# Layer 3 of a four-layer network: two outputs packed into one fp16 product of signs, another form of PReLU, and layer 2's norm folded into weights

## The chip, the cores and the metric

The kernel runs on one core of a Trainium2 chip. A core has five engines that run side by side and wait for one another through semaphores: TensorE (PE, matrix products into PSUM), VectorE (DVE), ScalarE (ACT), GpSimd (POOL) and SyncE (SP), which here issues nearly all the transfers. The metric is the device time of one execution in microseconds (us). Before the change it is 2025.56 us, the median of three runs from 2024.20 to 2026.01.

## What is computed

The input x has 8 images of 512 channels and 32 x 32 = 1024 pixels, in fp32. Four layers follow one another, each with a residual: an attention normed by the largest singular value (layer 0), a softmax attention over 512 channels (layer 1), one over 128 channels with a batch norm at its end (layer 2), and a binary convolution with PReLU (layer 3). The change touches the end of layer 2 and the whole of layer 3:

```python
# layer 2, its end: att is [n, 128, 1024]
z = einsum('oc,ncq->noq', Z_w, att)
inv = bn_gamma / sqrt(bn_var + 1e-5)
x = z * inv + (bn_beta - bn_mean * inv) + x

# layer 3; every vector has one value per channel
a = sign(x + rsign_bias)
scale = mean(abs(W), axis=1)
y = einsum('bchw,oc->bohw', a, sign(W) * scale)
bn = bn_gamma * (y - bn_mean) * rsqrt(bn_var + 1e-5) + bn_beta
t = bn + x - pr_shift
out = where(t > 0, t, pr_slope * t) + pr_bias
```

In layer 3 both operands of the product are signs, so that before scaling every output is a whole number between -512 and 512.

## The kernel before

Everything is laid out with channels on the 128 partitions: an image is four tiles of 128 channels (index cc or oc, 0 to 3) by 1024 pixels, and most work goes by halves of 512 pixels (index h). A product's output is a PSUM tile of 128 x 512, called `bank`; the main part has 8 of them.

A start of some 215 us loads the images, does layer 0's products (L1013), forms weights (`filler`, a list of small steps that is laid between the steps of the singular-value iteration, `chain`; in this part TensorE's order is written out by hand) and brings the first image into layer 1. Then `fast` is called for each of the 8 images in turn. For one image it does:

- `scores1`, `make_v`, `values1`: layer 1. The products follow the Strassen-Winograd scheme in `seven`, seven products in place of eight, so that each big product needs sums of quarters of its operands first. For the scores these sums are of u, made by `sums_of` on VectorE (L286 to L289, four additions of 128 x 1024).
- `project2`, `scores2` and the products with L799: layer 2's attention.
- `close2`: the product with Z (L632) into a bank, times the inverse of the softmax sums on VectorE (z, L637), the batch norm on ScalarE (L638, scale and bias per partition), the residual on GpSimd (L642).
- `leave`: layer 3. For each half, four Sign activations (L650) write the bf16 tile `sg`; for each of four output tiles four bf16 products (L660) fill one bank, and then come the scale and residual on VectorE (t, L670), Relu on ScalarE (up, L673), min(t + cb, 0) on VectorE (L674), slope times that plus up on VectorE (L675), the last bias on ScalarE (L678) and the store (L679).

The steps of `make_u` for the next image are handed out one by one between the steps of layers 2 and 3 (`fill`), so that TensorE has work while layer 2 and 3 wait for the other engines. After the last of them come the sums of u, and then the next image's `scores1`. The last image has no successor and so no such steps.

Outside the part with TensorE's order by hand, a planner lays out each engine's instructions: it takes them by their place in the program and by when, by its own costs, they could start. The program then holds one list for each engine, gone through in that order: in the trace, an instruction that waits holds up what is behind it.

Temporary tiles come from the pool `small`, three buffers for each tag: `half_a` holds t of layer 3 (and att, and the temporaries of `values1`), `half_b` holds z and `up`. A buffer is free again when its last reader is done; for a stored tile this is when the transfer has landed. In `leave` before the change the stored tile is `up`, in `half_b`.

Weights for layer 3 are made early: `sign_weights` writes the signs of W as bf16 (L958) and sums the absolute values, `scale_signs` makes the per-channel vectors sa3 (scale), cb3 (bias before PReLU), inv2 and bb2 (layer 2's norm). `biases` makes the biases of layer 1 by products with one column (L1089, L1104).

Of the kernel before, what the change touches and what calls it, by code (L numbers as in the profile page):

```python
# [8 lines left out]
F32 = mybir.dt.float32  # L9
BF16 = mybir.dt.bfloat16  # L10
I32 = mybir.dt.int32
# [60 lines left out]
GUARD = 1e20  # L72
RATIO = 8.0
EBUFS = 8


@with_exitstack
def kernel(
# [146 lines left out]
    gm = [keep.tile([P, 3, P], F32, tag=f"gm{j}", name=f"gm{j}") for j in range(NPAIR)]  # L225
    sw3 = wpool.tile([P, CC, C], BF16, tag="sw3", name="sw3")
    sa3 = const.tile([P, CC], F32, tag="sa3", name="sa3")
# [399 lines left out]

    def close2(env, xt, att, h, r=None):

        for oc in range(CC):  # L630
            ps = bank()
            mm(out=ps, lhsT=sbw["z"][:, bass.ts(oc, P)], rhs=att, start=True, stop=True)  # L632
            z = env["small"].tile([P, HF], F32, tag="half_b", name="z")
            if r is None:
                nc.scalar.copy(z, ps)
            else:
                nc.vector.tensor_tensor(z, ps, r, ALU.mult)  # L637
            nc.scalar.activation(  # L638
                z, z, AF.Identity, bias=bb2[:, oc : oc + 1], scale=inv2[:, oc : oc + 1]
            )  # L640
            xs = xt[:, oc, half(h)]
            nc.gpsimd.tensor_tensor(xs, xs, z, ALU.add)  # L642

    def leave(env, xt, dst, fill=lambda h: None):

        small = env["small"]
        for h in range(NH):
            sg = env["e"].tile([P, CC, HF], BF16, tag="e", name="sg")
            for cc in range(CC):
                nc.scalar.activation(  # L650
                    sg[:, cc, :],
                    xt[:, cc, half(h)],
                    AF.Sign,
                    bias=col("L3_conv_rsign_bias", cc),
                )
            for oc in range(CC):
                cb = cb3[:, oc : oc + 1]
                ps = bank()
                for cc in range(CC):
                    mm(  # L660
                        out=ps,
                        lhsT=sw3[:, cc, bass.ts(oc, P)],
                        rhs=sg[:, cc, :],
                        start=cc == 0,
                        stop=cc == CC - 1,
                    )

                t = small.tile([P, HF], F32, tag="half_a", name="t3")
                up = small.tile([P, HF], F32, tag="half_b", name="up3")
                nc.vector.scalar_tensor_tensor(  # L670
                    t, ps, sa3[:, oc : oc + 1], xt[:, oc, half(h)], ALU.mult, ALU.add
                )
                nc.scalar.activation(up, t, AF.Relu, bias=cb)  # L673
                nc.vector.tensor_scalar(t, t, cb, 0.0, ALU.add, ALU.min)  # L674
                nc.vector.scalar_tensor_tensor(  # L675
                    t, t, col("L3_conv_pr_slope", oc), up, ALU.mult, ALU.add
                )
                nc.scalar.activation(up, t, AF.Identity, bias=col("L3_conv_pr_bias", oc))  # L678
                nc.sync.dma_start(out=dst[:, oc, half(h)], in_=up)  # L679
                fill(h)  # L680

# [68 lines left out]
    def fast(env, n, hb, ua):  # L750
# [45 lines left out]
        for h in range(NH):  # L796
# [12 lines left out]
            if h == 0:  # L809
                r = inverse_sums(env, esum, B + n)  # L810
        close2(env, xt, atts[0], 0, r[:, 0, :])
        fill()
        close2(env, xt, atts[1], 1, r[:, 1, :])
        fill(2)
# [138 lines left out]
    def sign_weights():  # L953

        w3 = sbw["w3"]
        absw = a1.tile([P, 2, C], F32, tag="absw", name="absw")
        for cc in range(CC):
            nc.scalar.activation(sw3[:, cc, :], w3[:, cc, :], AF.Sign)  # L958
            nc.scalar.activation(absw[:, min(cc, 1), :], w3[:, cc, :], AF.Abs)
            if cc:  # L960
                nc.vector.tensor_tensor(absw[:, 0, :], absw[:, 0, :], absw[:, 1, :], ALU.add)
        return absw[:, 0, :]

    def scale_signs(total):
# [21 lines left out]
        nc.vector.tensor_tensor(bb2, inv2, vec("L2_conv_bn_mean"), ALU.mult)  # L986
        nc.vector.tensor_tensor(bb2, vec("L2_conv_bn_beta"), bb2, ALU.subtract)


# [201 lines left out]
    def filler():  # L1191

        yield from natural("v", "k")
        load_w("p", w_p, [P, CC, C], a1, tag="v")
        yield from gram(jl, 2, ht_pair[jl], gtl)
        yield from product(nat["q"], nat["k"], wu)
        cols2 = [slice(0, C // 2), slice(C // 2, C)]
        weights["u"] = sums_of(quarters_of(wu, chunks, cols2), [su[:, i] for i in range(3)])
        for j in rest:
            yield from grams(j)  # L1200
        yield from biases()
        yield from product(nat["v"], sbw["p"], wo)
        weights["o"] = sums_of(quarters_of(wo, chunks, cols2), [so[:, i] for i in range(3)])
# [176 lines left out]
    with tc.If(again > 0):  # L1380
        with (
            ExitStack() as stack,
            tc.tile_pool(name="gbig", bufs=1) as big,
            tc.tile_pool(name="gepool", bufs=2) as epool,
            tc.tile_pool(name="gsmall", bufs=1) as small,
        ):
# [50 lines left out]
```

## Time and profile before

| What | Value |
|---|---|
| time, median of 3 runs | 2025.56 us (2024.20 to 2026.01) |
| profiled execution, span | 2025.1 us, mean granted clock 0.988 |
| TensorE busy | 97% of the span |
| VectorE, ScalarE, GpSimd busy | 54%, 28%, 13% |
| transfers | 67.03 MB, 33 GB/s on average |
| one image, from the first layer-3 product to that of the next | about 219 us in the later images (1579.85 to 1798.51) |

The page of the profile has parts: the busy time of each engine; the span in 40 slices with the busy share in tenths and the clock granted to TensorE; the transfer queues; the chain of waits that ended last, with the share of each engine and line in it; and the groups of instructions, each with its line, engine, operation, output and inputs, count, busy time, the mean duration of one in ns, and the idle time of the engine just before them with what ended it. A fp32 product of 512 columns shows as two instructions. The durations of matmuls overlap, so that the cost of one in a stream is read from the distance between starts and not from its duration. The timeline lists one engine's instructions in order: start in us, time in us, engine, line, operation, output and inputs, shapes, count, and in brackets the idle time before it and what ended it.

### The profile page before, as it was taken

To read this page: it belongs to the slowest core of one execution; us is meant where nothing else is said; L and a number is where in the kernel's file an instruction comes from. 1 tells how busy PE (TensorE), PEld (TensorE's weight loads), DVE (VectorE), ACT (ScalarE), POOL (GpSimd) and SP (SyncE) were. 2 spreads that over 40 slices of the span, in tenths; PEclk is the share of its full clock that TensorE was granted. 3 is DMA by queue.
4 is the path that set the end of the run, shared out by engine and by line. 5 is a ranking of instruction groups with operands and counts; after the bars stand their busy time and mean duration, and the time that the engine had idled before them with its cause. 6 is when DMAs were issued, how large, how long until landed. Compare 5 with 4: busy or idle time off the path is not lost.

```text
span 2025.1 us, 17059 instructions
## 1 busy us (share of the span) xinstructions
PE 1956.3 (97%) x6358; PEld 1004.2 (50%) x6366; DVE 1090.0 (54%) x1801; ACT 571.5 (28%) x888; POOL 269.4 (13%) x215
## 2 busy tenths in 40 slices
PE   8989899999999999999999999999999999999995
PEld 2366346544655446443555446543644454544552
DVE  2254577337763587336653676247643665365435
ACT  2141132134222433025212431043202521242024
POOL 0000001111011200202020211120020202020111
PEclk9997999999999999999999999999999999999998
DMA  8320000002000020002000110002000200010001
GB/s 326 125 74 2 4 6 12 0 11 83 17 0 0 26 73 11 0 11 83 16 0 0 53 47 11 1 16 78 11 0 11 83 11 0 0 47 6 11 1 54
DMA packets 26715, 67.03 MB, mean 33 GB/s; under 512 B 3760, under 2 KB 4016, under 8 KB 25984
## 3 DMA queue, kind: packets, MB, share of 16 engines
q1 hardware_dynamic: 25968, 65.09, 9.5%
q8 instruction: 52, 0.85, 0.2%
q0 software_dynamic: 224, 0.33, 0.1%
q10 hardware_dynamic: 432, 0.43, 0.1%
q14 instruction: 39, 0.32, 0.1%
HBM read 38.51 MB, written 18.87 MB: 28 GB/s over the span
## 4 chain that ended last, share of the span: by engine, by line
PE 85%; DVE 7%; ACT 4%; POOL 2%; issue 1%; DMA 0%; ACTq 0%; POOLq 0%; DVEq 0%
PE bank L356 33%; PE bank L518 19%; PE bank L799 6%; PE bank L603 5%; PE bank L694 5%; PE bank L1013 4%; PE bank L615 3%; POOL xt L642 2%; DVE t L675 2%; PE bank L379 2%; PE wide L1069 1%; DVE t L670 1%; ACT z L638 1%; PE bank L1123 1%; PE bank L835 1%; DVE t L674 1%
## 5 line engine op out<-in xcount | busy, mean ns | idle before, releaser
L518 PE MATMUL bank<-e,vt 128*128 128x512 f32 x768 | 334.0, 593 | 0.0
L518 PEld LDWEIGHTS bank<-e,vt 128*128 128x128 f32 x768 | 145.1, 190 | 175.3 <-issue 171.6
L356 PE MATMUL bank<-ut,h 128*128 128x512 f32 x384 | 184.4, 600 | 8.2 <-ACT e L320 5.9
L356 PE MATMUL bank<-us,hs 128*128 128x512 f32 x256 | 122.4, 601 | 8.2 <-DVE us L287 8.2
L315 DVE TENSOR_TENSOR e<-bank,e 128x512 f32<-128x512 f32 x128 | 87.9, 686 | 64.7 <-PE bank L356 63.6
L356 PEld LDWEIGHTS bank<-ut,h 128*128 128x128 f32 x384 | 70.2, 190 | 93.4 <-issue 74.3
L642 POOL TENSOR_TENSOR xt<-xt,z 128x512 f32<-128x512 f32 x64 | 80.0, 1272 | 272.3 <-ACT z L638 161.0
L694 PE MATMUL bank<-tpg 128*128 128x512 f32 x256 | 114.6, 593 | 0.0
L603 PE MATMUL bank<-xt,tpg 128*128 128x512 f32 x256 | 113.6, 593 | 0.0
L799 PE MATMUL bank<-e,tpg 128*128 128x512 f32 x256 | 113.3, 596 | 0.0
L330 POOL TENSOR_TENSOR e<-e 128x512 f32<-128x512 f32 x32 | 41.0, 1280 | 467.5 <-ACT e L309 425.7
L701 ACT ACTIVATE e<-bank 128x512 f32<-128x512 f32 x128 | 76.4, 597 | 93.5 <-PE bank L694 93.5
L356 PE MATMUL bank<-h,wu 128*128 128x512 f32 x192 | 92.1, 603 | 6.3 <-DVE h L427 6.3
L356 PE MATMUL bank<-wo,h 128*128 128x256 f32 x384 | 91.8, 382 | 5.4 <-ACT vt L320 5.4
L315 DVE TENSOR_TENSOR vt<-bank,vt 128x512 f32<-128x512 f32 x64 | 43.7, 683 | 85.3 <-PE bank L356 84.1
L706 DVE TENSOR_TENSOR esum<-esum,e 128x1024 f32<-128x1024 f32 x48 | 58.8, 1226 | 54.8 <-ACT e L701 54.8
L723 DVE RECIPROCAL rsum<-bank 128x512 f32<-128x512 f32 x16 | 53.7, 3358 | 56.8 <-PE bank L715 56.5
L330 POOL TENSOR_TENSOR ut<-ut 128x512 f32<-128x512 f32 x16 | 23.9, 1493 | 449.7 <-ACT ut L311 244.2
L356 PEld LDWEIGHTS bank<-wo,h 128*128 128x128 f32 x384 | 71.9, 190 | 19.9 <-ACT vt L320 8.6
L637 DVE TENSOR_TENSOR z<-bank,rfull 128x512 f32<-128x512 f32 x64 | 44.3, 692 | 68.4 <-PE bank L632 51.7
L799 PEld LDWEIGHTS bank<-e,tpg 128*128 128x128 f32 x256 | 48.0, 190 | 63.9 <-issue 63.9
L356 PEld LDWEIGHTS bank<-us,hs 128*128 128x128 f32 x256 | 46.5, 190 | 65.6 <-issue 49.9
(288 smaller groups left out, 3078.4 us busy)
## 6 DMA issues: line engine op xcount, KB each, us to landing
xt<-in_x SPq DMA_DIRECT2D x56, 512.0 KB
out<-up SPq DMA_DIRECT2D x64, 256.0 KB
rfull<-rsum SPq DMA_DIRECT2D x64, 128.0 KB
f_dram<-f SPq DMA_DIRECT2D x8, 256.0 KB
fb<-f_dram SPq DMA_DIRECT2D x8, 256.0 KB
w<-in_w SPq DMA_DIRECT2D x1, 1024.0 KB
q<-in_w_q SPq DMA_DIRECT2D x1, 1024.0 KB
k<-in_w_k SPq DMA_DIRECT2D x1, 1024.0 KB
```

Of the source, the lines that this page charges most:

```text
L315: nc.vector.tensor_tensor(dst, ps, u, ALU.add)
L330: nc.gpsimd.tensor_tensor(c22, c22, c12, ALU.add)
L356: mm(out=ps[:, q * w : (q + 1) * w], lhsT=lt(ka, kb, q, k), rhs=rhs(ka, kb, q, k), start=first and q == 0 and k == 0, stop=last and k == 1 ...
L518: mm(out=ps, lhsT=a[:, t, bass.ts(r_, P)], rhs=e[t], start=first and t == 0, stop=last and t == NTH - 1, skip_group_check=True,)
L603: mm(out=ps, lhsT=sbw["tpg"][:, cc, bass.ts(i, P)], rhs=xt[:, cc, half(h)], start=cc == 0, stop=cc == CC - 1,)
L615: mm(out=ps[:, i, :], lhsT=xt[:, cc, bass.ts(4 * h + i, P)], rhs=sbw["tpg"][:, cc, 2 * P : 3 * P], start=cc == 0, stop=cc == CC - 1,)
L642: nc.gpsimd.tensor_tensor(xs, xs, z, ALU.add)
L694: mm(out=ps, lhsT=pt[:, 0, bass.ts(t, P)], rhs=tt[:, 0, half(h)], start=True, stop=True,)
L701: nc.scalar.activation(e[:, half(h)], ps, AF.Exp, scale=float(P) ** -0.5)
L706: nc.vector.tensor_tensor(esum, esum, e, ALU.add)
L799: mm(out=ps, lhsT=gt[:, t, :], rhs=es[t][:, half(h)], start=t == 0, stop=t == NT - 1,)
L1013: mm(out=banks[i][side(h), :], lhsT=w0[i][:, cc, :], rhs=xt[:, cc, half(h)], start=cc == 0, stop=cc == CC - 1,)
```

## The change

It has four parts.

1. **One product for two outputs.** The weights of output tile j (channels 0 to 255) and of tile j + 2 (256 to 511) are packed into one fp16 number: sign of the one plus 1026 times the sign of the other. These are whole numbers of at most 1027, which fp16 holds exactly. One product then gives y1 + 1026 y2 in a bank. ScalarE takes y2 out by scaling with 1/1026 and adding 1.5 x 2^23, which rounds to a whole number; VectorE subtracts that constant again and forms y1 as the bank less 1026 y2. Half the products of layer 3 are left.
2. **PReLU in another form.** In place of Relu plus slope times min(t, 0), it is (1 - slope) times Relu(t) plus slope times t, plus the bias. The Relu and the slope times t with both biases in it are on ScalarE, their sum is one VectorE operation, and its output is what is stored.
3. **Layer 2's norm folded.** The factor inv2 goes into Z's weights once at the start (`scale_z`, with four small products that turn it from a column into rows), the bias bb2 goes into the biases of layer 3's Sign and PReLU. The activation L638 falls away. In the last image half the residual additions go to VectorE.
4. **Order at the start.** `biases` runs ahead of the grams of layer 0's remaining pairs, with `scale_z` just before it.

The pool of the fallback path (`gsmall`), which runs only where a guard finds values out of range, has two buffers for each tag in place of one.

```diff
-    sw3 = wpool.tile([P, CC, C], BF16, tag="sw3", name="sw3")
+    sw3 = wpool.tile([P, CC, C // 2], F16, tag="sw3", name="sw3")
...
-    def close2(env, xt, att, h, r=None):
+    def close2(env, xt, att, h, r=None, last=False):
...
             z = env["small"].tile([P, HF], F32, tag="half_b", name="z")
-            if r is None:
-                nc.scalar.copy(z, ps)
-            else:
-                nc.vector.tensor_tensor(z, ps, r, ALU.mult)
-            nc.scalar.activation(
-                z, z, AF.Identity, bias=bb2[:, oc : oc + 1], scale=inv2[:, oc : oc + 1]
-            )
-            xs = xt[:, oc, half(h)]
-            nc.gpsimd.tensor_tensor(xs, xs, z, ALU.add)
+            nc.vector.tensor_tensor(z, ps, r, ALU.mult)
+            eng = nc.vector if last and oc % 2 else nc.gpsimd
+            eng.tensor_tensor(xs, xs, z, ALU.add)
...
-            for oc in range(CC):
-                cb = cb3[:, oc : oc + 1]
+            for j in range(CC // 2):
                 ps = bank()
                 for cc in range(CC):
                     mm(
                         out=ps,
-                        lhsT=sw3[:, cc, bass.ts(oc, P)],
+                        lhsT=sw3[:, cc, bass.ts(j, P)],
                         rhs=sg[:, cc, :],
...
-                t = small.tile([P, HF], F32, tag="half_a", name="t3")
-                up = small.tile([P, HF], F32, tag="half_b", name="up3")
-                nc.vector.scalar_tensor_tensor(
-                    t, ps, sa3[:, oc : oc + 1], xt[:, oc, half(h)], ALU.mult, ALU.add
-                )
-                nc.scalar.activation(up, t, AF.Relu, bias=cb)
-                nc.vector.tensor_scalar(t, t, cb, 0.0, ALU.add, ALU.min)
-                nc.vector.scalar_tensor_tensor(
-                    t, t, col("L3_conv_pr_slope", oc), up, ALU.mult, ALU.add
-                )
-                nc.scalar.activation(up, t, AF.Identity, bias=col("L3_conv_pr_bias", oc))
-                nc.sync.dma_start(out=dst[:, oc, half(h)], in_=up)
-                fill(h)
+                y2 = small.tile([P, HF], F32, tag="half_a", name="y2")
+                y1 = small.tile([P, HF], F32, tag="half_a", name="y1")
+                nc.scalar.activation(y2, ps, AF.Identity, bias=round3, scale=1.0 / PACK)
+                nc.vector.tensor_scalar(y2, y2, ROUND, None, ALU.subtract)
+                nc.vector.scalar_tensor_tensor(y1, y2, -PACK, ps, ALU.mult, ALU.add)
+
+                for y, oc in ((y1, j), (y2, j + 2)):
+                    nc.vector.scalar_tensor_tensor(
+                        y, y, sa3[:, oc : oc + 1], xt[:, oc, half(h)], ALU.mult, ALU.add
+                    )
+                    up = small.tile([P, HF], F32, tag="half_b", name="up3")
+                    nc.scalar.activation(up, y, AF.Relu, bias=cb3[:, oc : oc + 1])
+                    nc.scalar.activation(
+                        y,
+                        y,
+                        AF.Identity,
+                        bias=pb3[:, oc : oc + 1],
+                        scale=col("L3_conv_pr_slope", oc),
+                    )
+                    nc.vector.scalar_tensor_tensor(
+                        y, up, ps3[:, oc : oc + 1], y, ALU.mult, ALU.add
+                    )
+                    nc.sync.dma_start(out=dst[:, oc, half(h)], in_=y)
+                    fill(h)
...
-            nc.scalar.activation(sw3[:, cc, :], w3[:, cc, :], AF.Sign)
+            nc.scalar.activation(sign[:, cc, :], w3[:, cc, :], AF.Sign)
...
+        lo, hi = sign[:, :, 0 : C // 2], sign[:, :, C // 2 :]
+        nc.vector.scalar_tensor_tensor(sw3, hi, PACK, lo, ALU.mult, ALU.add)
...
+    def scale_z():
+
+        rep = a1.tile([P, CC, P], F32, tag="absw", name="rep")
+        nc.vector.tensor_copy(rep, inv2.unsqueeze(2).to_broadcast([P, CC, P]))
+        ps = bank()
+        for oc in range(CC):
+            mm(out=ps[:, bass.ts(oc, P)], lhsT=rep[:, oc, :], rhs=ident, start=True, stop=True)
+        nc.vector.tensor_tensor(sbw["z"], sbw["z"], ps, ALU.mult)
...
         weights["u"] = sums_of(quarters_of(wu, chunks, cols2), [su[:, i] for i in range(3)])
+        scale_z()
+        yield
+        yield from biases()
         for j in rest:
             yield from grams(j)
-        yield from biases()
```

The biases rb3, pb3 and the factor ps3 = 1 - slope are made by five more small VectorE operations in `scale_signs`.

## The prediction, made before the changed kernel ran

> **What bounds the kernel now.** I read the page from the top: share by engine, clock, the chain that ended last.
>
> ```profile
> PE 1956.3 (97%) x6358; PEld 1004.2 (50%) x6366; DVE 1090.0 (54%) x1801; ACT 571.5 (28%) x888; POOL 269.4 (13%) x215
> PEclk9997999999999999999999999999999999999998
> PE 85%; DVE 7%; ACT 4%; POOL 2%; issue 1%; DMA 0%; ACTq 0%; POOLq 0%; DVEq 0%
> L660 PE MATMUL bank<-sg,sw 128*128 128x512 bf16 x248 | 61.3, 379 | 3.5 <-ACT sg L650 3.0
> ```
>
> TensorE is never long without work and carries 85% of the chain; its clock is full. So a matmul removed from the stream counts at its spacing, unless the stream then waits elsewhere. The last line (groups of instructions) is the product that the change halves; 379 ns is one instruction with its latency, so the price must come from the spacing. For that and for what stands around it I take the timeline of one image's end, first TensorE, then VectorE:
>
> ```profile
> 1368.00 1.88 PE L356 MATMUL bank<-hs,wu 128*128 128x512 f32 x4
> 1369.72 3.62 PE L660 MATMUL bank<-sg,sw 128*128 128x512 bf16 x16
> 1373.17 1.88 PE L356 MATMUL bank<-ut,h 128*128 128x512 f32 x4
> 1375.89 1.98 PE L356 MATMUL bank<-ut,h 128*128 128x512 f32 x4 [0.84 <-ACT e L320]
> 1378.96 1.99 PE L356 MATMUL bank<-us,hs 128*128 128x512 f32 x4 [1.09 <-DVE us L287]
> 1381.41 1.98 PE L356 MATMUL bank<-ut,h 128*128 128x512 f32 x4 [0.47 <-DVE ut L288]
> ```
> ```profile
> 1373.20 2.06 DVE L670 SCALAR_TENSOR_TENSOR t<-bank,sa,xt 128x512 f32<-128x512 f32 x3
> 1375.18 0.87 DVE L674 TENSOR_SCALAR t<-t,cb 128x512 f32<-128x512 f32 x2
> 1375.97 1.41 DVE L675 SCALAR_TENSOR_TENSOR t<-t,ct,up 128x512 f32<-128x512 f32 x2
> 1377.29 0.48 DVE L674 TENSOR_SCALAR t<-t,cb 128x512 f32<-128x512 f32 x1
> 1377.69 1.22 DVE L287 TENSOR_TENSOR us<-us,ut 128x1024 f32<-128x1024 f32 x1
> ```
>
> Sixteen bf16 products start at 1369.72 and the next matmul at 1373.17: 3.45/16 = **0.216 us each**. Then the next image's scores begin and TensorE waits 0.84 + 1.09 + 0.47 = 2.40 us (1.92 in the first three images, where the singular-value chain fills the last gap; 15.4 us over seven image ends). Two of these waits are for the sums of u (L286 to L289), which stand on VectorE behind the PReLU of layer 3. So at this place VectorE is nearly a second bound.
>
> [...]the trace has 97 ns for bf16 against 190 for f32. No fp16 product is in this trace; I take bf16's price. [...]483 ns (L674) against 745 and 747 (L670, L675). [...]806 ns with scale and bias (L638), 711 with a bias (L673).
>
> **The change, part by part.**
>
> *Product.* 8 images x 2 halves x 4 outputs x 4 = 256 matmuls become 128. 128 x 0.216 = 27.6 us; 16 per image, 3.45 us. In seven images they stand in TensorE's stream: **-24.1 us**. The last image's are in the tail, where VectorE sets the end.
>
> *Layer 2's norm.* Eight L638 activations per image go, 8 x 0.806 = 6.45 us of ScalarE, and each z reaches GpSimd 0.8 us sooner. In seven images the signs of a half are done before TensorE comes to them (no wait at L660 there), so this is worth nothing on the path. In the tail it is: below.
>
> *Unpacking and PReLU, per pair of outputs.* Before, VectorE: 2 x (0.745 + 0.483 + 0.747) = 3.95 us; ScalarE: 2 x (0.711 + 0.720) = 2.86. After, VectorE: a subtract 0.48, the low output 0.745, then 2 x (0.745 + 0.747) = 4.21; ScalarE: rounding from PSUM 0.69 (L249), then 2 x (0.711 + 0.806) = 3.72. With four pairs, VectorE has 1.05 us more work per image and ScalarE 3.4 more, less the 6.45 above.
>
> *A new wait.* y1 and y2 both lie in the three half_a buffers until their store has landed; before, t was free after L675 and only `up` waited. A store takes about 2.1 us: in the tail one is issued at 2004.78 and L673, which waits for its buffer, starts at 2006.87. The second pair's y2 gets the third buffer, its y1 needs the first pair's y1 landed. From y1 to y1: low output 0.75, scale-add 0.75, Relu 0.71, scaled copy 0.81, last add 0.75, store 2.1, hand-overs 0.3 = **6.1 us per pair**, against 4.2 of VectorE work. If buffers are taken strictly in turn, y2's store counts and it is 7.6. Behind the blocked low output on VectorE stand the other PReLU steps, the sums of u and the additions of the scores.
>
> *At the image ends* this cuts both ways. Layer 3 takes four periods, 24.6 us, instead of about 23 (1360.5 to 1383.5), but each period leaves 1.9 us of VectorE free, and the sums (1.22 us each) fit there. By the order of readiness I get the second sum done near 1373 and the third near 1376, where before they were done at 1378.9 and 1381.4. TensorE comes to the scores at 1369.7, has two products of 1.72 us that need no sum (with 0.84 of wait between), and so needs the second sum at about 1374. I take **1.0 us of wait saved** per image end, -7 us: less than the 1.56 that this schedule gives, since queues are filled in advance and in order.
>
> *Tail.* Before, layer 3's first VectorE step is at 2000.35, since the signs stood behind L638 on ScalarE. After, additions split over GpSimd and VectorE give the four signs by about 1994.7 and the product by 1995.3; VectorE is free of z and additions at 1997.4. From a first low output at about 1998, three periods of 6.1 and 5.5 us to the last add end near 2021.8, where the last store is issued; before, the last issue was at about 2017.5 and the guard's count at 2019.2, with 5.85 us to the end of the span. So **+3 us**; without the buffer wait, -2.7.
>
> *Start.* Four transposing products (8 instructions of 0.11) and a copy and a product on VectorE for Z's scaling: about 1 us. Packing of signs, 1.3 us of VectorE, lies in layer 0's loop, where VectorE idles 2 to 6 us at a time. The biases move ahead of the grams: the same TensorE work; the waits they cause now (1.48 and 1.53 us at 174 and 183) recur earlier or vanish. **+1.5 us**, between -2 and +3.
>
> Sum: 2025.6 - 24.1 - 7 + 3 + 1.5 = **1999**.
>
> **Rivals.**
> 1. *VectorE takes the gain back and more.* The order of before is kept, the sums behind the same share of layer 3. From 1360.3 to 1385.0 VectorE was busy 21.4 of 24.7 us; with 1.05 more, the third sum comes some 0.9 us later than before and TensorE with it: +0.9 x 7 + 3 + 1.5 = **2036**. For it: two waits at the image ends are already VectorE's, and a longer PReLU stands in front. Against it: the new gaps.
> 2. *Half of it.* The sums come 1.5 us earlier than before, no more: -10.5 + 4.5 gives **2020**.
> 3. *All waits go.* The 15.4 us vanish and the stores don't hold the buffers: 2025.6 - 24.1 - 15.4 - 2.7 + 1.5 = **1985**. For it: ScalarE, whose copy makes the 0.84, loses 3 us per image. Against it: that copy follows its own product in any case.
>
> **How the numbers follow.** My forecast 0.60; half 0.17; all waits 0.12; slower 0.11. The range leaves out the slow rival and half of the best: 1984 to 2020, which also spans the start's and the tail's bounds around the forecast. Faster: 0.60 + 0.17 + 0.12 = 0.89; of the slow case 0.02 may land within 0.2%, 0.09 above.
>
> **What would show it.** L660's line at 128 matmuls and some 31 us busy; image ends 4 to 4.5 us closer together on TensorE; waits for the sums there under 2.4 us; VectorE's low-output line waiting for stores, about two microseconds a time; the first layer-3 step of the last image near 1998 and its last near 2022. Wrong would be: TensorE waiting over 4 us for L287's or L288's successors at each image end (rival 1), fp16 products spaced well above 0.216 us, or the scores' additions stuck behind a low output that waits for a store.

## The result, and the profile after

| | before | after |
|---|---|---|
| time, median | 2025.78 us (2024.20 to 2026.23, 4 runs) | 2007.53 us (2007.33 to 2008.71, 4 runs) |
| ratio | 1 | 0.9912, 95% interval 0.9895 to 0.9930 |
| profiled span | 2025.1 us | 2005.5 us |
| start, up to the first product of u | 215.0 | 212.0 |
| from there to the eighth image's first Z product | 1772.65 | 1749.9 |
| tail, from that product to the end | 37.4 | 43.6 |

The change gains 18 us, and the time is 8.5 us above the predicted one. The three lower rows are read from TensorE's timeline and add up: 3.0 gained in the start, 22.7 between, 6.2 lost in the tail. Below I call the middle part the images and the place between two of them an image end. Line numbers are now those of the changed kernel: L367 Strassen product (before L356), L297 to L300 the sums (before L286 to L289), L644 Z product, L650 z, L660 Sign, L666 packed product (before L660), L675 rounding, L676 subtraction, L677 low output, L680 scale and residual, L684 Relu, L685 slope copy, L692 last addition.

Of the changed kernel: busy time by engine, granted clock and chain by engine from the page, and the product's line from the groups of instructions:

```profile
PE 1930.2 (96%) x6246; PEld 999.1 (50%) x6246; DVE 1110.4 (55%) x1813; ACT 555.2 (28%) x856; POOL 262.6 (13%) x212
PEclk9989999999999999999999999999999999999997
PE 90%; DVE 6%; ACT 2%; issue 1%; DMA 1%; POOL 0%; DVEq 0%; ACTq 0%; POOLq 0%
L666 PE MATMUL bank<-sg,sw 128*128 128x512 f16 x128 | 31.7, 379 | 2.7 <-ACT sg L660 2.7
```

Half the products are left, at the same 379 ns (and 98 ns to load the weights of one, where the bf16 ones took 97), and TensorE's share of the chain is higher still. Nothing on the page tells that a gain was lost. It shows in the timeline of TensorE at the end of the fifth image:

```profile
1351.59 1.89 PE L666 MATMUL bank<-sg,sw 128*128 128x512 f16 x8
1353.32 1.88 PE L367 MATMUL bank<-ut,h 128*128 128x512 f32 x4
1357.58 1.98 PE L367 MATMUL bank<-us,hs 128*128 128x512 f32 x4 [2.38 <-DVE us L298]
1359.40 1.88 PE L367 MATMUL bank<-ut,h 128*128 128x512 f32 x4
```

Eight fp16 products take 1353.32 - 1351.59 = 1.73 us, 0.216 each. But before, the waits here were 0.84, 1.09 and 0.47, and now there is one of 2.38: the same sum in one piece. VectorE in the same place, in order:

```profile
1349.89 1.46 DVE L692 SCALAR_TENSOR_TENSOR y<-up,ps,y 128x512 f32<-128x512 f32 x2 [1.50 <-ACT y L685]
1351.26 0.75 DVE L328 SCALAR_TENSOR_TENSOR ut<-bank,bu,ut 128x512 f32<-128x512 f32 x1
1351.92 0.42 DVE L676 TENSOR_SCALAR y<-y 128x512 f32<-128x512 f32 x1
1352.26 1.22 DVE L297 TENSOR_TENSOR us<-ut 128x1024 f32<-128x1024 f32 x1
1353.39 0.68 DVE L677 SCALAR_TENSOR_TENSOR y<-y,bank 128x512 f32<-128x512 f32 x1
1353.99 0.75 DVE L328 SCALAR_TENSOR_TENSOR ut<-bank,bu,ut 128x512 f32<-128x512 f32 x1
1354.65 1.41 DVE L680 SCALAR_TENSOR_TENSOR y<-y,sa,xt 128x512 f32<-128x512 f32 x2
1355.97 0.42 DVE L676 TENSOR_SCALAR y<-y 128x512 f32<-128x512 f32 x1
1356.31 1.22 DVE L298 TENSOR_TENSOR us<-us,ut 128x1024 f32<-128x1024 f32 x1
```

From 1349.89 to the end of this stretch VectorE has no gap. The second sum (L298) stands behind the second pair's low output and scale-adds and the third pair's subtraction, and ends at 1357.53; TensorE starts 0.05 us later.

The tail, VectorE again (the figure in brackets is the idle time before the line and what ended it):

```profile
1973.57 0.69 DVE L677 SCALAR_TENSOR_TENSOR y<-y,bank 128x512 f32<-128x512 f32 x1
...
1977.54 1.46 DVE L692 SCALAR_TENSOR_TENSOR y<-up,ps,y 128x512 f32<-128x512 f32 x2 [1.49 <-ACT y L685]
1980.40 0.69 DVE L677 SCALAR_TENSOR_TENSOR y<-y,bank 128x512 f32<-128x512 f32 x1 [1.40 <-DMA out<-y]
...
1984.03 1.46 DVE L692 SCALAR_TENSOR_TENSOR y<-up,ps,y 128x512 f32<-128x512 f32 x2 [1.16 <-ACT y L685]
1986.92 0.69 DVE L677 SCALAR_TENSOR_TENSOR y<-y,bank 128x512 f32<-128x512 f32 x1 [1.43 <-DMA out<-y]
```

From low output to low output it is 6.83 and then 6.52 us, and each after the first waits for a store to land: the buffer wait of the prediction.

### The profile page after: what moved, and what is told of

Its sections match the earlier page's. It is cut to its first block, busy times and chain, and to the rows that moved or that the text cites. A ratio compares the mean times of both kernels' runs of the same rounds, so it can differ in the third digit from the quotient of the medians.

```text
span 2005.5 us, 16742 instructions
## 1 busy us (share of the span) xinstructions
PE 1930.2 (96%) x6246; PEld 999.1 (50%) x6246; DVE 1110.4 (55%) x1813; ACT 555.2 (28%) x856; POOL 262.6 (13%) x212
## 4 chain that ended last, share of the span: by engine, by line
PE 90%; DVE 6%; ACT 2%; issue 1%; DMA 1%; POOL 0%; DVEq 0%; ACTq 0%; POOLq 0%
PE bank L367 35%; PE bank L529 19%; PE bank L815 6%; PE bank L614 5%; PE bank L710 5%; PE bank L1048 4%; PE bank L626 3%; PE bank L644 3%; PE bank L390 2%; DVE y L680 2%; PE wide L1104 1%; PE bank L851 1%; PE bank L852 1%; PE bank L1158 1%; PE bank L731 1%
## 5 line engine op out<-in xcount | busy, mean ns | idle before, releaser
L367 PE MATMUL bank<-ut,h 128*128 128x512 f32 x384 | 183.9, 601 | 0.0
L367 PE MATMUL bank<-us,hs 128*128 128x512 f32 x256 | 124.7, 610 | 17.2 <-DVE us L298 17.2
L367 PEld LDWEIGHTS bank<-ut,h 128*128 128x128 f32 x384 | 71.9, 193 | 82.9 <-issue 78.7
L652 POOL TENSOR_TENSOR xt<-xt,z 128x512 f32<-128x512 f32 x60 | 75.3, 1286 | 261.8 <-DVE z L650 261.8
L341 POOL TENSOR_TENSOR e<-e 128x512 f32<-128x512 f32 x32 | 42.3, 1323 | 447.9 <-ACT e L320 436.1
L367 PE MATMUL bank<-h,wu 128*128 128x512 f32 x192 | 92.1, 603 | 6.2 <-DVE h L438 6.2
L367 PE MATMUL bank<-wo,h 128*128 128x256 f32 x384 | 91.8, 382 | 5.4 <-ACT vt L331 5.4
L367 PEld LDWEIGHTS bank<-us,hs 128*128 128x128 f32 x256 | 47.0, 193 | 75.2 <-issue 47.4
L367 PEld LDWEIGHTS bank<-wo,h 128*128 128x128 f32 x384 | 72.0, 190 | 19.8 <-ACT vt L331 8.6
L341 POOL TENSOR_TENSOR ut<-ut 128x512 f32<-128x512 f32 x16 | 20.5, 1283 | 457.6 <-ACT ut L322 457.6
L710 PEld LDWEIGHTS bank<-tpg 128*128 128x128 f32 x256 | 48.7, 191 | 60.6 <-issue 58.5
```

The source lines that it names most:

```text
L341: nc.gpsimd.tensor_tensor(c22, c22, c12, ALU.add)
L367: mm(out=ps[:, q * w : (q + 1) * w], lhsT=lt(ka, kb, q, k), rhs=rhs(ka, kb, q, k), start=first and q == 0 and k == 0, stop=last and k == 1 ...
L652: eng.tensor_tensor(xs, xs, z, ALU.add)
L710: mm(out=ps, lhsT=pt[:, 0, bass.ts(t, P)], rhs=tt[:, 0, half(h)], start=True, stop=True,)
```

## The experiments

My theory after the result: TensorE and VectorE race to the second sum at each image end, and what packing takes from TensorE is worth only as much as the sum comes sooner; in the tail the stored buffers cost it. The rivals were that the buffer wait, the clock, or simply the place of the sums in the program was to blame, and, most awkward, that packing was not where the gain came from. "Ratio" is to the kernel before, with its 95% interval.

### 1. No packing (e_nopack)

```diff
-            for j in range(CC // 2):
+            for oc in range(CC):
...
-                nc.scalar.activation(y2, ps, AF.Identity, bias=round3, scale=1.0 / PACK)
-                nc.vector.tensor_scalar(y2, y2, ROUND, None, ALU.subtract)
-                nc.vector.scalar_tensor_tensor(y1, y2, -PACK, ps, ALU.mult, ALU.add)
...
-                        y, y, sa3[:, oc : oc + 1], xt[:, oc, half(h)], ALU.mult, ALU.add
+                        y, ps, sa3[:, oc : oc + 1], xt[:, oc, half(h)], ALU.mult, ALU.add
```

> The changed kernel with its first part undone: 256 fp16 products with plain signs, four outputs per half, no rounding and no unpacking; the new PReLU, the folded norm and the order at the start stay. Theory A (TensorE is the bound; the products are worth their spacing and the waits at the image ends stay): +24.1 us at seven image ends, tail some 8 us shorter since VectorE has 5 us less to do and y is held by one store each: 2007.5 + 24.1 - 8 = about 2024. Rival B (VectorE is nearly the bound there, so that the unpacking costs what the products save): the 2.4 us wait for the second sum vanishes at each image end, 2024 - 17 = about 2007.

Measured: 1999.07 us (4 runs, from 1995.61 to 2001.74), ratio 0.9865 (0.9850 to 0.9880), under both theories, though the wait vanished as rival B said. So in this kernel **packing is a loss of about 8.5 us** by the medians; the two profiled executions are 5.6 us apart, and they show where that comes from: 112 more products, 24.1 us, stand in the images' stream and lengthen it by only 2.8 us (1752.75 against 1749.92), and the tail is 35.2 against 43.6 us. TensorE at the fifth image's end, without packing:

```profile
1355.55 3.62 PE L666 MATMUL bank<-sg,sw 128*128 128x512 f16 x16
1359.00 1.88 PE L367 MATMUL bank<-ut,h 128*128 128x512 f32 x4
1360.72 1.88 PE L367 MATMUL bank<-us,hs 128*128 128x512 f32 x4
```

There is no wait for the sum: the products that packing removes cover it.

### 2. PReLU alone, and the fold alone (e_prelu, e_fold)

If packing loses, the other parts must gain more than the whole. Both kernels are the one before with a single part of the change (the fold without the last image's split of additions between GpSimd and VectorE).

```diff
-                nc.vector.tensor_scalar(t, t, cb, 0.0, ALU.add, ALU.min)
-                nc.vector.scalar_tensor_tensor(
-                    t, t, col("L3_conv_pr_slope", oc), up, ALU.mult, ALU.add
-                )
-                nc.scalar.activation(up, t, AF.Identity, bias=col("L3_conv_pr_bias", oc))
-                nc.sync.dma_start(out=dst[:, oc, half(h)], in_=up)
+                nc.scalar.activation(
+                    t, t, AF.Identity, bias=pb3[:, oc : oc + 1], scale=col("L3_conv_pr_slope", oc)
+                )
+                nc.vector.scalar_tensor_tensor(t, up, ps3[:, oc : oc + 1], t, ALU.mult, ALU.add)
+                nc.sync.dma_start(out=dst[:, oc, half(h)], in_=t)
```

> The kernel before with the new form of the PReLU alone (slope copy on ScalarE in place of the bias copy, one VectorE operation fewer per output); 256 products, layer 2's norm and the order of the start stay. Theory A (the PReLU's form, about 4 us of VectorE per image, is what lets the sums come in time at image ends in the unpacked kernel, where the time from the first product of u to the eighth image fell by 20 us): about 2025 - 18 = 2007, between 2003 and 2012, and PE's wait for the second sum gone. Theory B (the fold of the norm, which takes 8 copies per image from ScalarE and the sums' rivals from the queue, did it): 2020 to 2026, waits at image ends as before.

Measured: 2008.74 us (4 runs), ratio 0.9914 (0.9898 to 0.9931); the images' part is 1753.77 us, 18.9 less than before, the tail 38.3. The new form alone, with one VectorE operation fewer per output, is worth 16.7 us, nearly what the whole change is worth. It also moves a copy on ScalarE ahead of the last addition and stores another tile; which of these counts most isn't separated.

```diff
-            nc.scalar.activation(
-                z, z, AF.Identity, bias=bb2[:, oc : oc + 1], scale=inv2[:, oc : oc + 1]
-            )
...
-                    bias=col("L3_conv_rsign_bias", cc),
+                    bias=rb3[:, cc : cc + 1],
```

> The kernel before with only layer 2's norm folded into weights and biases (8 copies per image on ScalarE gone, scaling of z's weights in the step of the sums; the old PReLU, 256 products, biases after the grams). The prediction took this part as worth nothing on the path inside the images. Theory A (right): the tail is shorter by the first copy's and the last additions' share, 1 to 5 us, image ends as before: 2020 to 2025. Theory B (ScalarE's relief lets Sign and so layer 3 begin earlier at each image end, and part of the wait goes): 2007 to 2016.

Measured: 2020.79 us (12 runs), ratio 0.9977 (0.9968 to 0.9986): 3.7 us in the images and 2.4 in the tail of its profile. The time is in theory A's span, but what it says of the image ends isn't quite right: the second sum comes half a microsecond sooner at each.

Now the race can be put in one table, read off the timelines of the fifth image's end, in us after that image's first Z product. "Needed" is when TensorE would have started the second sum's product had it never waited: one product of 1.72 us after the last product of signs. (In the kernel before and with the fold alone TensorE's queue has a second product in between, so that only a part of the lateness shows there as waits.)

| kernel | second sum ends | needed |
|---|---|---|
| before | 31.5 | 27.5 |
| fold alone | 31.0 | 27.5 |
| PReLU alone | 27.2 | 27.5 |
| no packing | 27.0 | 27.5 |
| after | 26.6 | 24.1 |

The PReLU's form brings the sum 4.3 us sooner, just ahead of the need. Packing moves the need by 3.45 us and the sum by 0.4.

### 3. Packed products without the unpacking (e_nounpack)

```diff
-                nc.scalar.activation(y2, ps, AF.Identity, bias=round3, scale=1.0 / PACK)
-                nc.vector.tensor_scalar(y2, y2, ROUND, None, ALU.subtract)
-                nc.vector.scalar_tensor_tensor(y1, y2, -PACK, ps, ALU.mult, ALU.add)
...
-                        y, y, sa3[:, oc : oc + 1], xt[:, oc, half(h)], ALU.mult, ALU.add
+                        y, ps, sa3[:, oc : oc + 1], xt[:, oc, half(h)], ALU.mult, ALU.add
```

> The changed kernel keeps its 128 packed products, but both outputs are computed straight from the product's bank: the rounding copy, the subtraction and the low output are left out (their arithmetic is missing, so what is written differs from the reference's by that part). With the products as few as in the changed kernel, this takes 3 operations per pair away (1 on ScalarE, 2 on VectorE, about 0.6 and 1.1 us). Theory A (TensorE sets the time at image ends and only the unpacking keeps the packed form from paying): the wait for the second sum goes as in the unpacked kernel, and the 112 products saved show in full: 1999 - 24 = 1975, between 1970 and 1982. Theory B (what stands behind the wait is the chain layer 3, then fill, then sums, in time and not in VectorE's load: fewer products only bring TensorE sooner to a sum that isn't ready): the wait stays near 2 us per image, about 1986 to 2000.

Measured: 1988.17 us (4 runs), ratio 0.9813 (0.9797 to 0.9829), in the span of theory B, while the wait was smaller than B said. The images' part is 12.2 us under the unpacked kernel's, half of the 24.1. TensorE at the fifth image's end:

```profile
1349.82 1.88 PE L367 MATMUL bank<-ut,h 128*128 128x512 f32 x4
1352.49 1.98 PE L367 MATMUL bank<-ut,h 128*128 128x512 f32 x4 [0.80 <-ACT e L331]
1354.67 1.98 PE L367 MATMUL bank<-us,hs 128*128 128x512 f32 x4 [0.19 <-DVE us L298]
```

The second sum ends 27.1 after the first Z product here, no sooner than in the unpacked kernel, and is needed at 24.1 as in the change. The planner fills most of the gap with another product (that of 1352.49), and here two short waits are left; from 430 to 1960 us they sum to 8.5. So of the 21.3 us that packing fails to bring in the images (24.1 less 2.8), leaving out the unpacking brings back 9.4 (12.2 less 2.8); the other 11.9 are missing even with the unpacking free.

### 4. The pair in buffers that don't wait (e_pair, e_bufs4)

```diff
-                y2 = small.tile([P, HF], F32, tag="half_a", name="y2")
-                y1 = small.tile([P, HF], F32, tag="half_a", name="y1")
+                pair = env["e"].tile([P, 2, HF], F32, tag="e", name="pair")
+                y2, y1 = pair[:, 1, :], pair[:, 0, :]
```

> The changed kernel with y1 and y2 of a pair in one tile of the score tiles' pool (eight tiles of 128 x 1024) in place of the three half_a buffers, so that no low output waits for a store. Theory A (the store wait costs only in the tail; at the image ends it lets the sums of u in between layer 3's steps): tail about 6.5 us shorter, but the second sum of u now stands behind all four pairs on VectorE, TensorE waits some 5 us longer at each of seven image ends, time about 2007.5 - 6.5 + 30 = 2031. Rival B (the store wait is a pure cost, at the image ends as well): 2007.5 - 6.5 in the tail and up to 1 us per image end, about 1995 to 2001.

Measured: 2029.79 us (9 runs), ratio 1.0023 (1.0013 to 1.0033). The tail is 35.2 us, 8.4 shorter, as the buffer wait would have it; but the images' part is 32.2 us longer. TensorE's waits in this kernel from 430 to 1960 us (total, times, longest):

```profile
PE bank L367 <- ACT e L331: 17.6, 7, 2.5
PE bank L367 <- DVE us L298: 7.2, 7, 2.1
PE bank L666 <- ACT sg L660: 6.4, 14, 0.7
```

**Inside the images the buffer wait was a help.** It doesn't stand where the prediction put it: in the changed kernel VectorE's low outputs wait for stores in the tail alone (three times, 4.2 us), while at each image end ScalarE's rounding of the fourth pair waits 3.4 us, 23.8 in all:

```profile
L675 ACT ACTIVATE y<-bank,round 128x512 f32<-128x512 f32 x32 | 21.8, 682 | 44.7 <-DMA out<-y 23.8 <-DVE us L297 12.6 <-DVE y L677 5.9
```

So the low outputs of the last two pairs come late, and the sums stand on VectorE ahead of them. With the pair's tile all four low outputs and scale-adds stand ahead of the second sum, which ends 32.2 after the first Z product, not 26.6, and the evacuation L331 of the next image's first bank stands in ScalarE's queue behind Relus and slope copies:

```profile
1378.21 0.57 ACT L331 COPY e<-bank 128x512 f32<-128x512 f32 x1
```

The product that it copies ended near 1376.3, so in this trace the copy stood 1.9 us behind what was ahead of it in the queue, and ScalarE had no gap in that time.

TensorE's clock has a part in it too. In the 30 us from 20 us after the first Z product, the granted clock is 0.89 to 0.94 at six of seven image ends; in the changed kernel it is 0.94 at two and 1.00 at five. By these shares (an estimate: what is missing to 1.00, times 30 us, is 13.8 us here and 3.6 there) some 10 of the 32.2 us are the clock's.

The same with a fourth buffer and the tiles where they were (the tag's other tiles get four as well):

```diff
-                y2 = small.tile([P, HF], F32, tag="half_a", name="y2")
-                y1 = small.tile([P, HF], F32, tag="half_a", name="y1")
+                y2 = small.tile([P, HF], F32, tag="half_a", name="y2", bufs=4)
+                y1 = small.tile([P, HF], F32, tag="half_a", name="y1", bufs=4)
```

> The changed kernel with four buffers in place of three for the tiles that y1 and y2 come from, and nothing else. Theory A (a pair's rounding waits for the store of the pair before, since three buffers hold one pair and a half; a pair in a tile of its own took 8.4 us off the tail and cost 32 us at image ends, where the wait had let the sums in): four buffers hold two pairs, the tail is shorter by 4 to 8 us, and the image ends are longer, by up to 32 us: 2006 to 2030, with the tail below 40 us. Theory B (it was the pool and not the number: the pair's tile changed what the exponentials wait for): tail 43 to 44 as in the changed kernel, and 2006 to 2009.

Measured: 2009.47 us (4 runs), ratio 0.9919 (0.9904 to 0.9934): tail 36.9, 6.7 shorter; images' part 1760.2, 10.3 longer. So in the tail it is the number of buffers that counts, and a fourth one buys nothing on the whole. In the images it brings a third of what the pair's tile costs, and not by the second sum, which ends at 26.6 as in the change: the third sum now stands behind another pair (TensorE waits 2.0 us for it), TensorE's other waits from 430 to 1960 us are 3.2 us longer together, and the clock is down at four image ends instead of two.

### 5. The sums issued ahead of layer 3 (e_early35)

`make_u` has 15 steps, 14 with products and at last the sums. Seven are handed out before the Z products. The two numbers that the edits below change say how many follow after the additions of each half: with 1 and 2, as in the change, the sums come after all of layer 3, with 3 and 5 ahead of it.

```diff
         close2(env, xt, atts[0], 0, r[:, 0, :], not more)
-        fill()
+        fill(3)
         close2(env, xt, atts[1], 1, r[:, 1, :], not more)
-        fill(2)
+        fill(5)
```

> The changed kernel with the steps of the next image's u handed out earlier: three instead of one after close2 of half 0, five instead of two after close2 of half 1, so that the sums of u come in the program before layer 3. The same work. Theory A (the 2.4 us at each image end are the second sum's place behind layer 3 on VectorE): the wait goes, 7 x 2.4 = 16.7 us less, about 1991. Rival B (VectorE has too much to do there in any order): the wait moves to the scores' additions, time within 4 us of 2007.5.

Measured: 2004.48 us (4 runs), ratio 0.9896 (0.9881 to 0.9912), some 3 us under the change, as rival B said. The wait for L298 is gone, and others stand in its place (TensorE's waits, as above):

```profile
PE bank L367 <- ACT ut L322: 8.4, 7, 1.2
PE bank L410 <- DVE mv L409: 4.3, 4, 1.4
PE bank L367 <- DVE e L326: 2.3, 2, 1.3
```

All of TensorE's waits over this stretch sum to 23.0 us, against 23.6 in the change, so they have moved and not gone. What has gone is the drops of the clock: it is 1.00 in the 30-us windows of all seven image ends, and the two drops of the change cost some 3.4 us (section 8).

### 6. Both together (e_pair_early35, e_late35, e_late24)

If the buffer wait only helped because the sums stood behind it, it can go once they stand in front. First the edits of e_pair and e_early35 together:

```diff
+                pair = env["e"].tile([P, 2, HF], F32, tag="e", name="pair")
+                y2, y1 = pair[:, 1, :], pair[:, 0, :]
...
-        fill(2)
+        fill(5)
```

> Two edits of the changed kernel together: the pair y1, y2 in one tile of the pool of exponentials (tail -8.4 alone, but the sums came too late at image ends, +32), and the sums' steps issued ahead of layer 3 (fill 3 and 5 after the two halves' additions, in place of 1 and 2). Theory A (the two are independent: the sums are out of the way of the pairs by then): start 211, from u to the eighth image 1747, tail 35: about 1994, between 1990 and 1999. Theory B (the pair's tile and the next image's exponentials come from the same pool, so that the exponentials now wait for the stores): TensorE waits at each image end for an exponential's tile, 2003 to 2030.

Measured: 1999.05 us (4 runs), ratio 0.9867 (0.9850 to 0.9883). The tail is 35.2 and the later images take 215.4 and 213.6 us each, but the first two take 237.75 and 228.84 against 230.99 and 223.98 with small buffers. TensorE's longest wait from 443 to 560 us in this kernel points to the reason:

```profile
PE bank L367 <- DVE r L914: 3.2, 1, 3.2
```

r belongs to the singular-value chain of the other samples, which runs beside the first two images and also works on VectorE; now it stands behind layer 3. So the pair's own tile is used from the third image on:

```diff
+                if paired:
+                    pair = env["e"].tile([P, 2, HF], F32, tag="e", name="pair")
+                    y2, y1 = pair[:, 1, :], pair[:, 0, :]
+                else:
                     y2 = small.tile([P, HF], F32, tag="half_a", name="y2")
                     y1 = small.tile([P, HF], F32, tag="half_a", name="y1")
...
-        leave(env, xt, channels(out[b]), lambda h: fill(1 - h))
+        leave(env, xt, channels(out[b]), lambda h: fill(1 - h), n > 1)
```

> The changed kernel with the sums issued ahead of layer 3 (fill 3 and 5) and with the pair y1, y2 in one tile of the pool of exponentials only from the third image on. In the first two images the products of the chains for the next samples' norms wait on VectorE, and with pair tiles in them those two images took 237.75 and 228.84 us against 230.99 and 223.98 with three small buffers; in the later images the pair tiles took 0.8 us off per image, 215.4 and 213.6 against 216.5 and 215.9. Theory A (the buffer's wait is a matter of who goes first on VectorE: chains in the first two images, the sums later): the two gains add, eighth image at 897.6 + 215.4 + 213.6 + 215.4 + 213.6 + 196.1 = 1951.7, tail 35.2, span 1986.9: about 1987, between 1984 and 1991. Theory B (what is taken from the first images comes back later, because the chains' products that are left over fall into the third and fourth image): 1993 to 1999.

Measured: 1987.29 us (5 runs), ratio 0.9812 (0.9798 to 0.9825); its eighth image began at 1950.6, where theory A had 1951.7. And with 2 and 4 steps in place of 3 and 5:

```diff
-        fill(3)
+        fill(2)
         close2(env, xt, atts[1], 1, r[:, 1, :], not more)
-        fill(5)
+        fill(4)
```

> As the kernel with fills 3 and 5, but all four steps of the sums after the second half's additions (fill 0 and 4), so that ScalarE isn't busy with the copies of u when Sign is due (TensorE waited there 1.4 us per image for sg). Theory A (that wait goes and nothing takes its place): 7 x 1.4 less than the other, about 1978. Theory B (the sums are then ready later, and TensorE waits for them or for the copies of u): 1987 to 1996.

The expectation speaks of 0 and 4; the kernel that ran has 2 and 4. So 13 steps come ahead of layer 3, and the sums stand in the program behind its first pair of outputs.

Measured: **1984.95 us** (5 runs), ratio 0.9797 (0.9784 to 0.9811), the best of all and 23 us under the change. It landed between the two theories, but with another order than theirs it decides neither. TensorE's wait for sg stayed (8.4 us in all, against 6.9 with 3 and 5), and the gain came from the first two images, which took 229.43 and 222.19 us against 230.88 and 224.04. VectorE at the fifth image's end:

```profile
1340.57 0.75 DVE L328 SCALAR_TENSOR_TENSOR ut<-bank,bu,ut 128x512 f32<-128x512 f32 x1 [4.53 <-PE bank L367]
1341.36 1.22 DVE L297 TENSOR_TENSOR us<-ut 128x1024 f32<-128x1024 f32 x1
1342.50 0.42 DVE L680 TENSOR_SCALAR pair<-pair 128x512 f32<-128x512 f32 x1
1342.84 1.22 DVE L298 TENSOR_TENSOR us<-us,ut 128x1024 f32<-128x1024 f32 x1
```

In this stretch only one subtraction of layer 3 is ahead of L298 (in this kernel L680 is the subtraction). The sum ends 20.9 after the first Z product, and its product starts at 25.2, without a wait.

### 7. Is it the packing, then? (e_nopack24)

The kernel without packing of experiment 1, with one more edit:

```diff
-        fill()
         close2(env, xt, atts[1], 1, r[:, 1, :], not more)
-        fill(2)
+        fill(4)
```

> The kernel with 256 separate fp16 products (no packing; new PReLU, fold and start kept) with the sums' four steps after the second half's additions, as in the kernel with fills 0 and 4. It tells whether the packing is what brings 1999 to 1985, or the new order alone. Theory A (the unpacked kernel had no wait of TensorE at image ends, so the order has nothing to take away, and the 112 products more, 24.1 us, stand in full): 1998 to 2004. Theory B (the order is worth the same without packing): 1985 to 1992.

Here the sums come behind the first half of layer 3. Measured: 1998.99 us (4 runs), ratio 0.9862 (0.9846 to 0.9879): this order gives the unpacked kernel nothing, since its TensorE had no wait for the sums to lose. From 430 to 1960 us it waits only 6.8 us (6.7 in e_nopack), so that no order could give it much.

The best packed kernel is 1998.99 - 1984.95 = 14.0 us under this one, 13.5 of it in the images (1737.3 against 1750.8). That is what packing, an order made for it and the pair's tile are worth together: the two kernels differ in all three, and an unpacked kernel with 2 and 4 was not run. As the change had it, packing cost 8.5.

### 8. The start's order back (e_bias)

```diff
         scale_z()
-        yield
-        yield from biases()
         for j in rest:
             yield from grams(j)
+        yield from biases()
```

> The changed kernel with the order at the start undone: biases after the grams of the remaining pairs as before the change, scale_z in the step of the sums. Theory A (the order of the biases gave the start its 3 us): first product of u at about 215 us instead of 212 us, time about 2010.5 to 2011.5. Rival B (the start gained for another cause, so the order is worth nothing): within 1 us of 2007.5.

Measured: 2016.41 us (5 runs), ratio 0.9957 (0.9943 to 0.9971), above both theories. The start is 3.6 us longer: the order is worth what the start gained. But the images' part is longer too, by 4.7 (and the tail by 0.8), with the same 2.38 us wait at each image end. What differs is TensorE's clock. Four-microsecond windows of the changed kernel at the sixth image's end, with the wait in the first (the third column from the right is the granted clock):

```profile
1570.00:1574.00 4.00, 1.62 (x4) 0.49 (x3) 4.00 (x6) 2.77 (x5) 0.00 (x0) 1.00 0.01 2
1574.00:1578.00 4.00, 4.00 (x7) 1.73 (x6) 3.63 (x5) 0.60 (x3) 0.00 (x0) 0.59 0.34 131
```

After the wait the clock is down, and that image took 216.25 us where one without the drop took 214.57: 1.7 us. In windows of 0.1 us the clock reads 0.50 from 1574.7 to 1578.1, and 3.4 us at half speed cost 1.7. In the profile of the change it is so at two of seven image ends; with the old start order at five. Three more drops of 1.7 us are 5.1, near the 4.7 seen.

## Why the prediction was right, and where it was off

The direction held, and so did the price of a product: 2007.5 lies in the range, 1999 was 8.5 us too low. That it came so near is in part luck. Of the 24.1 us that the products save, 21.3 did not arrive in the images, and the PReLU's form, which the sum counted as no gain, brought 18.9 there; the two nearly cancel. In the profiled spans the steps sum to 2025.1 - 24.1 + 1.4 + 6.2 - 3.0 = 2005.6.

| step | forecast | measured |
|---|---|---|
| products, seven images | -24.1 | -24.1 (by their number, at the measured 0.216 us each) |
| waits at the image ends | -7 | +1.4 (what remains of -22.7) |
| tail | +3 | +6.2 |
| start | +1.5 | -3.0 |

**The step that failed is the wait at the image ends.** I had the second sum ready near 1373 in the time of before, 25.6 after the first Z product, and needed near 1374, 26.6 after it. It came at 26.6, one microsecond later, and was needed at 24.1, since TensorE's new queue has one product ahead of it that needs no sum, not two. So the whole 2.4 us of wait stayed, in one piece, where I had 1.0 saved, and the drops of the clock (two of 1.7 us) came on top. The gaps that I saw on VectorE were real only at the first pair (1.50 idle before 1349.89); then it has none. Rival 1's mechanism, VectorE as the second bound at this place, was thus nearer the truth than the chance of 0.11 that I gave it, but its size wasn't: it saw a longer PReLU and not that the new form has one VectorE operation fewer per output; this form alone is worth 16.7 us. I counted unpacking and PReLU as one sum of +1.05 us per image on VectorE, and by this hid a large gain and a larger loss in each other.

The waits of before sum to 15.9 us, not 15.4: the last of the three is missing at the first two image ends, not at three. In the change they are 16.7. With the two drops of the clock that is 4.2 us more, while the row says +1.4, so some 2.8 us were gained elsewhere in the images; where isn't shown.

**Layer 2's norm.** "Worth nothing on the path" inside the images was wrong by about half a microsecond per image end; the fold alone gives 4.7 us, tail included.

**The tail.** The mechanism was right: low outputs wait for stores, and without the wait the tail is 8.4 us shorter. The size was off by 3.2: the first low output came 11.7 after the first Z product where I had 10.3, and the periods are 6.83, 6.52 and 6.50, not 6.1 (my own terms sum to 6.17; the 0.3 in them for hand-overs is an estimate: six like the 0.05 from the end of L287 at 1378.91 to TensorE's start at 1378.96 give it), for ScalarE does both Relus of a pair before the first slope copy. Forecast without the wait: -2.7 against before; measured, with the pair's tile: 37.4 to 35.2, -2.2.

**The start.** I left open whether the two waits of 1.48 and 1.53 us recur or vanish, and -3.0 lies outside my span of -2 to +3. They vanished: before, the products of one column (L1089, L1104) stood at the end of the chain, and the copies of their results held VectorE's queue; the granted clock was 0.50 from 172 to 184 us and 0.86 from 184 to 212, and after the change 1.00 and 0.95. But from 138 to 172 it was 0.99 before and 0.75 after: the slow stretch came earlier and was only some 3 us shorter (0.50 from 171.2 to 191.6 before, from 141.1 to 158.2 after). What of the gain is the clock's isn't shown.

**What would show it** came true for the product's line (31.7 us busy) and, in the later images where the clock held, for the image ends (closer by 4.1 to 4.6 us). The low outputs wait for stores in the tail alone, 1.4 us rather than two, and the wait for the sums at an image end is 2.38 us, just under the 2.4 of the sign but more than the 1.56 of before. What would have made it wrong didn't come: no wait over 4 us at an image end.

What sets off the drops of the clock isn't shown. The two in the changed kernel last 3.4 us each, at 0.50; one begins 1.2 us after the wait of 2.38 us has ended, the other just as it ends, and at the other five image ends the same wait has no drop after it. I moved the images in time only by way of the start's order, so why the drops fell at just those ends isn't shown either.

## What to carry to other kernels

Work taken off the bounding engine is worth only the slack of the next operand it needs: write down for that place when the operand is ready and when it is needed, and move its producer ahead of other work first. Then test each part of a compound change alone: here the headline part cost 8.5 us as delivered, and the packed kernel came 14.0 under the unpacked one only after its sums and its buffers had been moved, while a small rewrite beside it made the gain. And a wait that a profile shows may be what keeps a queue in a good order; taking it away can cost more than it did.

## What the runs showed of the hardware

At all seven image ends of the changed kernel TensorE has a single wait of 2.38 or 2.39 us; at two of them the granted clock then falls to 0.50 for 3.4 us, which cost 1.7 us each time, and with the old order of the start it falls at five. In the trace of before, three waits that sum to as much (2.40) have no drop after them: the clock reads 1.00 from 230 to 1990 us.

At 1345.97 in the changed kernel two scale-adds (L680) took 2.43 us instead of 1.41, while GpSimd added from 1346.55 to 1347.85 (L341): the first took 0.75, and the second, begun at 1346.64, 1.76. Ten of the 64 scale-adds took 1.76 us, and each of them began 0.09 to 0.12 us after such an addition; the 14 others that overlap one began before it and took 0.75. Before, the scale-add (L670) read its first operand from a bank, and all 64 took 0.74 to 0.75, among them 15 that began while GpSimd was adding. The unpacking brings that operand into SBUF; that this makes the difference is my reading of the two traces, and no run here tested or priced it by itself.
